# Whole-row taps of the last convolution tiles moved to ScalarE and added by transfers, in a kernel of attention and 7x7 depthwise convolution

## The chip, the cores and the metric

The kernel runs on one core of a Trainium2 chip. Times are microseconds of device time for one execution. The kernel before took 2925.66 us, the median of three runs.

## The reference

The input x has 16 images of 384 channels and 32 x 32 pixels in float32. Two layers follow each other, both with a residual and a GroupNorm of 32 groups ahead (`_gn`; its scale is one and its shift is zero):

```
x = x + attention(_gn(x))       # 8 heads of 48, 1024 tokens, softmax, projection with bias
x = x + depthwise_7x7(_gn(x))   # one 7x7 filter per channel, made symmetric under rotation
```

The filter is the mean of the weight and its three rotations by 90 degrees. The convolution pads with three zeros on each side, so its 49 taps (dy, dx) run from -3 to 3 in both directions, and a tap with dy = 2 touches 30 of the 32 rows.

## The kernel before

**Tiles.** The 384 channels are three tiles k = 0, 1, 2 of 128 partitions, each with the 1024 pixels of one image along the free dimension (512 KB). A tile is named (b, k), so that (15, 0) is the first tile of the last image. Attention works on four units (pairs of heads) per image. TensorE is busy with it nearly all the time: scores (L469), values times scores (L485), q and k (L418), v (L444), projection (L538). ScalarE takes the exponentials (L477) and copies results out of PSUM. The projection is added to x by an accumulating transfer issued on POOL (L553), which gives the tile `x1`.

**The convolution on VectorE.** It runs one image behind attention. `conv_begin` applies the GroupNorm to x1 and gives `xn1`. `conv_tap` (L600) is one instruction per tap: it multiplies a shifted window of xn1 by one weight per channel and adds it into x1. When the 49 taps of a tile are done, `conv_end` (L610) stores it from POOL's queue.

**The last tiles.** After the last attention unit there is nothing left to hide a convolution behind, so the last six tiles are shared out:

- (14, 2), (15, 2) and (15, 1), `PE_TILES`, go to TensorE. `conv_store` (L674) writes xn1 to a padded scratch in HBM, `conv_load` (L681) reads it back as tiles `sh` in which shifted rows lie on other partitions (four transfers of 160 KB, two each from SP's and ScalarE's queues in the tail), and `conv_on_pe` (L704) multiplies them by matrices made of the weights: seven column shifts dx, in two groups d0 of rows, 14 groups for each half of the image. For (14, 2) and (15, 2), `conv_on_pe_end` copies the sum out on ScalarE (L719), adds it into x1 by an accumulating transfer on POOL (L720), and stores. For (15, 1), `conv_on_pe_half` adds each half on VectorE (L727) and stores it (L728).
- (14, 0), (14, 1) and (15, 0) stay on VectorE. The last of them, `LONE`, alternates between two accumulators, x1 and `sum2`[...]; L858 starts sum2 and L866 joins the two at the end.

**Order.** The program is one long sequence that a planner in the kernel's Python code writes out. `clock` is its estimate of TensorE's time and `vclock` of VectorE's; `catch_up` issues taps until vclock reaches clock, and work that is due later sits in the heap `later`, each entry with a due time and a cost in microseconds. `applies` holds work for ScalarE that `act_slot` puts between exponentials. `fast_finish` writes the last projection of an image, its divisions included (L566 holds the reciprocal that VectorE takes first), and sets vclock anew. `fast_end` computes the statistics of the last x1 on TensorE (L308, with L327 and L330 on VectorE and the power L329 on POOL), applies them (L336 on VectorE and on POOL, L340 on ScalarE) and starts the last chains. Every engine, and every engine's transfer queue, works in the order in which it was written: an instruction that waits holds back all that stand behind it on that engine. Buffers come from pools: `epool` 8, `opool` 6, `npool` 6 for xn1, `tpool` 2.

Of the kernel before, what the change touches and what calls it, by code (L numbers as in the profile page):

```python
# [10 lines left out]
F32 = mybir.dt.float32  # L11
I32 = mybir.dt.int32
AF = mybir.ActivationFunctionType
ALU = mybir.AluOpType
AX = mybir.AxisListType

P = 128
# [27 lines left out]
def kernel(  # L45
# [25 lines left out]
    nc = tc.nc  # L71

    B, C, H, W = x.shape
    N = H * W
    NK = C // P
# [3 lines left out]
    HALF = N // 2  # L79
    KS = w_conv.shape[2]  # L80
    PAD = KS // 2
# [6 lines left out]
    TAPS = sorted(  # L88
        ((i - PAD, j - PAD) for i in range(KS) for j in range(KS)), key=lambda t: t != (0, 0)
    )  # L90
# [3 lines left out]
    wsym = consts.tile([P, NK, KS, KS], F32, name="wsym")  # L94
# [15 lines left out]
    def run(general):  # L110
        tag = "g" if general else "f"
        with ExitStack() as stack:
# [26 lines left out]

            PE_TILES = [(B - 2, PE_K[0])] + [(B - 1, k) for k in PE_K]  # L140
            LONE = (B - 1, 0)

            def flat(t):
                return t.rearrange("p h n -> p (h n)")
# [441 lines left out]
                )  # L586


            def region(*ds):
                return [(slice(max(0, -d), H - max(0, d)), slice(max(0, d), H - max(0, -d))) for d in ds]  # L590

            def conv_begin(st, b, k, engine):
                xn1s[b, k] = npool.tile([P, N], F32, tag="xn1", name=f"xn1_{b}_{k}")
                st.apply(xn1s[b, k], x1s[b, k], k, engine)

            def conv_tap(b, k, dy, dx, dst=None):
                (oy, iy), (ox, ix) = region(dy, dx)
                dst = x1s[b, k] if dst is None else dst
                acc = dst.rearrange("p (h w) -> p h w", w=W)[:, oy, ox]
                nc.vector.scalar_tensor_tensor(  # L600
                    acc,
                    xn1s[b, k].rearrange("p (h w) -> p h w", w=W)[:, iy, ix],
                    wsym[:, k, dy + PAD, dx + PAD : dx + PAD + 1],
                    acc,
                    ALU.mult,
                    ALU.add,
                )

            def conv_end(b, k):
                nc.gpsimd.dma_start(  # L610
                    out[b, k * P : (k + 1) * P].rearrange("p h w -> p (h w)"), x1s.pop((b, k))
                )
# [63 lines left out]
            def conv_load(b, k, h, a):  # L676
# [11 lines left out]
                    )  # L688
                shs[b, k, h, a] = t

            def conv_on_pe(b, k, h, first, last):
                if (b, k) not in pss:
                    pss[b, k] = psum(f"ps_conv_{b}_{k}")
                order = sorted(
                    ((d0, dx) for d0 in range(2) for dx in range(-PAD, PAD + 1)),
                    key=lambda t: t[1] != 0,
                )
                for n, (d0, dx) in enumerate(order):
                    if not first <= n < last:
                        continue  # L700
                    _, (ox, ix) = region(0, dx)
                    for i in range(SH):
                        src = shs[b, k, h, i // 2][:, i % 2, 0 : ROWS * W]
                        nc.tensor.matmul(  # L704
                            pss[b, k][CH * i : CH * (i + 1), h, :].rearrange(
                                "p (y x) -> p y x", x=W
                            )[:, :, ox],
                            lhsT=mats[k][:, i, d0 * KS + dx + PAD, :],
                            rhs=src.rearrange("p (y x) -> p y x", x=W)[
                                :, SH * d0 : SH * d0 + H // 2, ix  # L710
                            ],
                            start=(n == 0),
                            stop=(n == len(order) - 1),
                        )

            def conv_on_pe_end(b, k):

                t = tpool.tile([P, N], F32, tag="t", name=f"conv_{b}_{k}")
                nc.scalar.copy(t, flat(pss.pop((b, k))))  # L719
                nc.gpsimd.dma_start(x1s[b, k], t, accum_op=ALU.add)  # L720
                conv_end(b, k)

            def conv_on_pe_half(b, k, h):

                c = slice(h * HALF, (h + 1) * HALF)
                dst = x1s[b, k][:, c]
                nc.vector.tensor_tensor(dst, pss[b, k][:, h, :], dst, ALU.add)  # L727
                (nc.gpsimd, nc.sync)[h].dma_start(  # L728
                    out[b, k * P : (k + 1) * P].rearrange("p h w -> p (h w)")[:, c], dst
                )  # L730
# [88 lines left out]
            def now():  # L819
                return vclock if catching else max(clock, vclock)  # L820

            def after(wait, cost, f):

                nonlocal count
                count += 1
                heapq.heappush(later, (now() + wait, count, cost, f))

            def us_tap(dy, dx):
                late_us = 0.02 if clock > last_image else 0.0
                return ((H - abs(dy)) * (W - abs(dx)) + (128 if len(active) > 1 else 268)) / 955 + late_us  # L830

            def tap():

                while len(active) < NK and chains:
                    active.append([*chains.popleft(), 0])
                if not active:
                    return 0.0
                b, k, n = active[0]
                if (b, k) == LONE:
                    active.append(active.pop(0))  # L840
                    return tap_of_two(b, k, active[-1])
                took = us_tap(*TAPS[n])
                conv_tap(b, k, *TAPS[n])
                c = active.pop(0)
                c[2] += 1
                if c[2] < len(TAPS):
                    active.append(c)
                else:
                    conv_end(b, k)
                return took  # L850

            def tap_of_two(b, k, c):

                n = c[2]
                c[2] += 1
                if n == 1:
                    late["sum2"] = opool.tile([P, N], F32, tag="o", name=f"sum2_{b}_{k}")
                    nc.vector.tensor_scalar(  # L858
                        late["sum2"], xn1s[b, k], wsym[:, k, PAD, PAD : PAD + 1], None, ALU.mult
                    )  # L860
                elif n < len(TAPS):

                    tn = n if n > 1 else 1
                    conv_tap(b, k, *TAPS[tn], late["sum2"] if n % 2 else None)
                else:
                    nc.vector.tensor_tensor(x1s[b, k], x1s[b, k], late["sum2"], ALU.add)  # L866
                    active.remove(c)
                    conv_end(b, k)
                return (950 + 128) / 955

            def catch_up(to):
                nonlocal vclock, catching
# [114 lines left out]
                    f()  # L987

            def x1_chains(b, st):
                on_pe = [t for t in PE_TILES if t[0] == b]  # L990
                for k in range(NK - 1, -1, -1):
                    conv_begin(st, b, k, (nc.gpsimd, None, nc.vector)[k] if b == B - 1 else None)
                    if (b, k) in on_pe:
                        conv_store(b, k)

                        cuts = (0, KS, KS + 2, KS + 4, 2 * KS) if b == B - 2 else (0, KS, 2 * KS)
                        pe_conv.extend((b, k, 0, *c) for c in zip(cuts, cuts[1:]))
                        pe_conv.extend((b, k, 1, n, n + KS) for n in (0, KS))
                after(
                    2.0 if b == B - 1 else 6.0,  # L1000
                    0.0,
                    lambda: chains.extend(
                        (b, k) for k in range(NK) if (b, k) not in on_pe
                    ),
                )
# [114 lines left out]
            def conv_piece():  # L1120
                nonlocal clock
                b, k, h, first, last = pe_conv.popleft()
                while (b, k, h, 1) not in shs and pe_loads:
                    loads(1)
                conv_on_pe(b, k, h, first, last)
                clock += 6.2 * (last - first) / KS
                if last == 2 * KS:
                    loads(2)
                    if (b, k) == PE_TILES[-1]:
                        after(6.0, 0.7, lambda: conv_on_pe_half(b, k, h))  # L1130
                    elif h == 1:
                        after(6.0, 1.2, lambda: conv_on_pe_end(b, k))
# [29 lines left out]
                vclock = clock + 4.0  # L1162

            def fast_end(b):

                x1_stats[b].groups_on_pe(late["masks"], tap, conv_piece)
                conv_piece()
                x1_chains(b, x1_stats[b])
# [140 lines left out]
```

## Time and profile before

| what | us |
|---|---|
| median of three runs | 2925.66 |
| lowest, highest of them | 2924.74, 2926.32 |
| profiled execution, own time | 2926.36 |
| profiled execution, span of the core | 2924.6 |
| TensorE busy (share of the span) | 2895.0 (99%) |
| VectorE busy | 2580.3 (88%) |
| ScalarE busy | 1441.0 (49%) |
| POOL busy | 254.2 (9%) |
| transfers by POOL, queue q0, share of 16 engines | 14.7% |

The span is what the trace shows of the core, from its first to its last instruction; the execution's own time is 1.8 us more. All times in the timelines count from the start of the span. The last stage begins near 2832, when attention's matmuls end, and lasts to 2924.6. A row of a timeline gives the start, the duration, the engine, the line, the operation and its tiles, and in brackets how long the engine was idle before it and what ended that. A transfer's row gives the time that its issue took on the queue; the views of transfers give the time from issue to landing.

### The profile page before, as it was taken

To read this page: it belongs to the slowest core of one execution; us is meant where nothing else is said; L and a number is where in the kernel's file an instruction comes from. 1 tells how busy PE (TensorE), PEld (TensorE's weight loads), DVE (VectorE), ACT (ScalarE), POOL (GpSimd) and SP (SyncE) were. 2 spreads that over 40 slices of the span, in tenths; PEclk is the share of its full clock that TensorE was granted. 3 is DMA by queue.
4 is the path that set the end of the run, shared out by engine and by line. 5 is a ranking of instruction groups with operands and counts; after the bars stand their busy time and mean duration, and the time that the engine had idled before them with its cause. 6 is when DMAs were issued, how large, how long until landed. Compare 5 with 4: busy or idle time off the path is not lost.

```text
span 2924.6 us, 30111 instructions
## 1 busy us (share of the span) xinstructions
PE 2895.0 (99%) x11442; PEld 1164.5 (40%) x11442; DVE 2580.3 (88%) x2571; ACT 1441.0 (49%) x1721; POOL 254.2 (9%) x400
## 2 busy tenths in 40 slices
PE   8999999999999999999999999999999999999997
PEld 4343343433434343343433434343343434434332
DVE  5312999989899898999989899898999989899988
ACT  2545445464454655445464454556445464554520
POOL 3111004010100101000010100101010010100000
PEclk9999999999999999999999999999999999999999
DMA  7422022120312203012220302203022220302314
GB/s 281 131 29 62 16 35 76 37 68 23 68 29 43 69 21 84 16 35 69 42 63 23 72 29 39 70 21 84 16 41 64 43 62 24 80 24 35 104 53 128
DMA packets 72059, 168.93 MB, mean 58 GB/s; under 512 B 30288, under 2 KB 32224, under 8 KB 70368
## 3 DMA queue, kind: packets, MB, share of 16 engines
q0 software_dynamic: 32688, 109.34, 14.7%
q1 hardware_dynamic: 37936, 54.94, 7.4%
q10 hardware_dynamic: 1280, 2.62, 0.3%
q8 instruction: 92, 1.51, 0.2%
q14 instruction: 63, 0.52, 0.1%
HBM read 118.61 MB, written 28.72 MB: 50 GB/s over the span
## 4 chain that ended last, share of the span: by engine, by line
PE 92%; issue 5%; DVE 2%; DMA 0%; POOL 0%; ACT 0%; POOLq 0%
PE ps_s L469 29%; PE acc L485 29%; PE ps_qk L418 17%; PE ps_v L444 9%; PE ps_proj L538 8%; DVE x L600 1%; DVE sum L600 1%; DMA x<-in_x 0%; PE warm L1060 0%; PE ps_st_x L308 0%; ACT qk L425 0%; POOL v L180 0%; POOL qk L434 0%; POOL sc_x L329 0%; POOL x L1241 0%
## 5 line engine op out<-in xcount | busy, mean ns | idle before, releaser
L600 DVE SCALAR_TENSOR_TENSOR x<-xn,wsym,x 128x899 f32<-128x899 f32 (+9 forms) x2181 | 2375.7, 1162 | 138.7 <-ACT xn L340 138.7
L477 ACT ACTIVATE e<-ps_s 128x1024 f32<-128x1024 f32 x1024 | 952.4, 1051 | 52.2 <-PE ps_s L469 49.1
L469 PE MATMUL ps_s<-qk 48*128 48x512 f32 x4096 | 914.8, 596 | 1.3 <-ACT qk L425 1.1
L485 PE MATMUL acc<-e,v 128*64 128x512 f32 x4096 | 907.2, 595 | 0.0
L469 PEld LDWEIGHTS ps_s<-qk 48*128 48x128 f32 x4096 | 375.9, 185 | 536.4 <-ACT e L477 259.6
L485 PEld LDWEIGHTS acc<-e,v 128*64 128x64 f32 x4096 | 283.0, 137 | 608.2 <-issue 600.8
L418 PE MATMUL ps_qk<-x,wqk 128*128 128x512 f32 x1152 | 508.7, 598 | 2.4 <-DVE x L336 2.4
L496 ACT COPY o<-acc 128x512 f32<-128x512 f32 x128 | 75.1, 587 | 604.7 <-PE acc L485 604.7
L418 PEld LDWEIGHTS ps_qk<-x,wqk 128*128 128x128 f32 x1152 | 217.2, 191 | 290.1 <-issue 287.6
L444 PE MATMUL ps_v<-wv,x 128*128 128x384 f32 x768 | 252.0, 488 | 0.0
L538 PE MATMUL ps_proj<-o,wp 128*128 128x512 f32 x540 | 234.2, 592 | 0.0
L425 ACT COPY qk<-ps_qk 128x1024 f32<-128x1024 f32 x96 | 96.9, 1009 | 263.6 <-PE ps_qk L418 263.6
L553 POOL DMA_DIRECT2D x<-in_x x45 | 39.4, 875 | 1803.0 <-ACT x L546 1424.3
L444 PEld LDWEIGHTS ps_v<-wv,x 128*128 128x128 f32 x768 | 144.6, 190 | 109.6 <-ACT e L477 12.1
L538 PEld LDWEIGHTS ps_proj<-o,wp 128*128 128x128 f32 x540 | 102.6, 190 | 126.0 <-issue 119.6
L453 ACT COPY v<-ps_v 128x384 f32<-128x384 f32 x128 | 55.1, 483 | 185.5 <-PE ps_v L444 185.5
L546 ACT ACTIVATE x<-ps_proj,bp 128x1024 f32<-128x1024 f32 x45 | 50.2, 1114 | 182.7 <-PE ps_proj L538 182.7
L521 DVE TENSOR_TENSOR o<-o,inv 128x1024 f32<-128x1024 f32 x63 | 76.8, 1219 | 51.0 <-DMA inv<-inv 46.5
L340 ACT ACTIVATE xn<-x,sc_x 128x1024 f32<-128x1024 f32 x46 | 53.8, 1231 | 80.3 <-DMA sc_x<-gr_x 57.0
L704 PE MATMUL ps_conv<-sh,mat 128*32 128x464 f32 (+3 forms) x672 | 69.2, 570 | 1.9 <-DVE x L727 1.9
L363 DVE BATCH_NORM_STATS2 bs_all<-xs 128x6 f32<-128x512 f32 x84 | 52.2, 683 | 18.2 <-DMA xs<-in_x 18.2
L510 DVE RECIPROCAL rec<-sums 128x16 f32<-128x16 f32 x63 | 15.3, 243 | 53.6 <-DMA sums<-sum 53.5
(123 smaller groups left out, 556.6 us busy)
## 6 DMA issues: line engine op xcount, KB each, us to landing
x<-in_x POOLq DMA_DIRECT2D x90, 512.0 KB, 5.6
inv<-inv SPq DMA_DIRECT2D x126, 256.0 KB
out<-x POOLq DMA_DIRECT2D x47, 512.0 KB, 3.8
xs<-in_x POOLq DMA_DIRECT2D x42, 512.0 KB, 6.5
qk<-qk POOLq DMA_DIRECT2D x96, 128.0 KB, 5.8
o<-o SPq DMA_DIRECT2D x90, 64.0 KB
sh<-xd SPq DMA_DIRECT2D x32, 160.0 KB
x<-in_x SPq DMA_DIRECT2D x6, 512.0 KB
```

Of the source, the lines that this page charges most:

```text
L418: nc.tensor.matmul(ps[:, h, :], lhsT=wqk[:, k, s, t, :], rhs=xns[b][:, k, h * HALF : (h + 1) * HALF], start=(k == 0), stop=(k == NK - 1),)
L425: nc.scalar.copy(halves(qks[u][:, s, :]), ps)
L444: nc.tensor.matmul(ps[:, j, 0:C], lhsT=xns[b][:, k, t * P : (t + 1) * P], rhs=wv[:, k, :], start=(k == 0), stop=(k == NK - 1),)
L453: nc.scalar.copy(dst.rearrange("p (h d) -> p h d", d=D + 1)[:, :, 0:D], ps[:, j, 0:C].rearrange("p (h d) -> p h d", d=D),)
L469: nc.tensor.matmul(ps[:, j, :], lhsT=qks[u][r, 1, i * P : (i + 1) * P], rhs=qks[u][r, 0, h * HALF : (h + 1) * HALF], start=True, stop=True,)
L477: nc.scalar.activation(es[n], ps, AF.Exp, scale=SCALE)
L485: nc.tensor.matmul(accs[u, h][64 * j : 64 * j + 64, :], lhsT=v_of(u, i, j), rhs=e[:, j, :], start=(i == 0), stop=(i == NT - 1),)
L496: nc.scalar.copy(os_[u][:, h * HALF : (h + 1) * HALF], accs.pop((u, h)))
L521: nc.vector.tensor_tensor(os_[u], os_[u], invs.pop(u), ALU.mult)
L538: nc.tensor.matmul(ps[:, h, :], lhsT=wp[:, t, o * P : (o + 1) * P], rhs=os_[NP * b + t][:, h * HALF : (h + 1) * HALF], start=(t == 0), sto ...
L600: nc.vector.scalar_tensor_tensor(acc, xn1s[b, k].rearrange("p (h w) -> p h w", w=W)[:, iy, ix], wsym[:, k, dy + PAD, dx + PAD : dx + PAD + 1],
L704: nc.tensor.matmul(pss[b, k][CH * i : CH * (i + 1), h, :].rearrange("p (y x) -> p y x", x=W)[:, :, ox], lhsT=mats[k][:, i, d0 * KS + dx + ...
```

## The change

A tap with dx = 0 covers whole rows: its product is one contiguous run, weight times xn1 shifted by dy rows. The change takes such taps (`ROWS_ONLY`) off TensorE and VectorE. ScalarE computes the product into a buffer (`product`), and an accumulating transfer from POOL's queue adds it into the tile (`add_rows`).

- The three PE_TILES give up dy = 1, 2, 3. `PE_TAPS` therefore has 13 groups, not 14 (the second row group at dx = 0 is gone). For (14, 2) the three products are made during the last attention, in buffers of xn1 that are still spare (`rows_early`); for (15, 2) and (15, 1) in the tail, in two buffers of opool and one of npool each.
- (14, 1) gives up dy = -1, 1, 2, with products made before the last apply.
- LONE gives up all seven taps with dx = 0. Two products start sum2 and a new accumulator `sum3` (`lone_sums`); five are added into sum3 by transfers, one after the other. At the end VectorE adds sum3 to sum2 and sum2 to x1, in halves, each stored at once, one from SP's queue and one from ScalarE's.
- `add_step` works through the additions of the four tiles in turn, one from each. The sum of a tile on TensorE is taken only after its additions are written (`late["pe"]`), and (14, 1) is stored after its third addition.
- The apply of (15, 0) moves from POOL to ScalarE.
- `vclock -= 5.0` makes the planner place more taps ahead of the last image's reciprocals.

VectorE's taps in the whole program go from 2204 to 2195, and those behind the last apply from 60 to 48. The diff without its asserts and blank lines:

```diff
@@ -139,6 +139,13 @@
     PE_TILES = [(B - 2, PE_K[0])] + [(B - 1, k) for k in PE_K]
     LONE = (B - 1, 0)
+    ROWS_ONLY = {bk: (1, 2, 3) for bk in PE_TILES}
+    ROWS_ONLY[B - 2, 1] = (-1, 1, 2)
+    ROWS_ONLY[LONE] = range(-PAD, PAD + 1)
+    def taps_of(b, k):
+        return [t for t in TAPS if t[1] or t[0] not in ROWS_ONLY.get((b, k), ())]
     def flat(t):
         return t.rearrange("p h n -> p (h n)")
@@ -586,11 +593,27 @@
         )
+    spare = {}
+    def new_xn1(b, k):
+        return npool.tile([P, N], F32, tag="xn1", name=f"xn1_{b}_{k}")
+    def product(dst, b, k, dy):
+        rows, src = ((slice(i.start * W, i.stop * W)) for i in region(dy)[0])
+        nc.scalar.activation(
+            dst[:, rows],
+            xn1s[b, k][:, src],
+            AF.Identity,
+            scale=wsym[:, k, dy + PAD, PAD : PAD + 1],
+        )
+        return dst[:, rows], rows
     def region(*ds):
         return [(slice(max(0, -d), H - max(0, d)), slice(max(0, d), H - max(0, -d))) for d in ds]
     def conv_begin(st, b, k, engine):
-        xn1s[b, k] = npool.tile([P, N], F32, tag="xn1", name=f"xn1_{b}_{k}")
+        xn1s[b, k] = spare.pop((b, k), None) or new_xn1(b, k)
         st.apply(xn1s[b, k], x1s[b, k], k, engine)
     def conv_tap(b, k, dy, dx, dst=None):
@@ -688,14 +711,14 @@
             )
         shs[b, k, h, a] = t
+    PE_TAPS = [(d0, dx) for d0 in range(2) for dx in range(-PAD, PAD + 1) if d0 == 0 or dx]
+    PE_TAPS.sort(key=lambda t: t[1] != 0)
     def conv_on_pe(b, k, h, first, last):
         if (b, k) not in pss:
             pss[b, k] = psum(f"ps_conv_{b}_{k}")
-        order = sorted(
-            ((d0, dx) for d0 in range(2) for dx in range(-PAD, PAD + 1)),
-            key=lambda t: t[1] != 0,
-        )
-        for n, (d0, dx) in enumerate(order):
+        for n, (d0, dx) in enumerate(PE_TAPS):
             if not first <= n < last:
                 continue
             _, (ox, ix) = region(0, dx)
@@ -710,11 +733,12 @@
                         :, SH * d0 : SH * d0 + H // 2, ix
                     ],
                     start=(n == 0),
-                    stop=(n == len(order) - 1),
+                    stop=(n == len(PE_TAPS) - 1),
                 )
     def conv_on_pe_end(b, k):
         t = tpool.tile([P, N], F32, tag="t", name=f"conv_{b}_{k}")
         nc.scalar.copy(t, flat(pss.pop((b, k))))
         nc.gpsimd.dma_start(x1s[b, k], t, accum_op=ALU.add)
@@ -722,6 +746,7 @@
     def conv_on_pe_half(b, k, h):
         c = slice(h * HALF, (h + 1) * HALF)
         dst = x1s[b, k][:, c]
         nc.vector.tensor_tensor(dst, pss[b, k][:, h, :], dst, ALU.add)
@@ -839,12 +864,15 @@
         if (b, k) == LONE:
             active.append(active.pop(0))
             return tap_of_two(b, k, active[-1])
-        took = us_tap(*TAPS[n])
-        conv_tap(b, k, *TAPS[n])
+        taps = taps_of(b, k)
+        took = us_tap(*taps[n])
+        conv_tap(b, k, *taps[n])
         c = active.pop(0)
         c[2] += 1
-        if c[2] < len(TAPS):
+        if c[2] < len(taps):
             active.append(c)
+        elif (b, k) in ROWS_ONLY:
+            late["done"] = (b, k)
         else:
             conv_end(b, k)
         return took
@@ -853,20 +881,82 @@
         n = c[2]
         c[2] += 1
-        if n == 1:
-            late["sum2"] = opool.tile([P, N], F32, tag="o", name=f"sum2_{b}_{k}")
-            nc.vector.tensor_scalar(
-                late["sum2"], xn1s[b, k], wsym[:, k, PAD, PAD : PAD + 1], None, ALU.mult
-            )
-        elif n < len(TAPS):
-            tn = n if n > 1 else 1
-            conv_tap(b, k, *TAPS[tn], late["sum2"] if n % 2 else None)
+        taps = taps_of(b, k)
+        if n < len(taps):
+            conv_tap(b, k, *taps[n], late["sum2"] if n % 2 else None)
+        elif n == len(taps):
+            dst = late["sum2"]
+            nc.vector.tensor_tensor(dst, dst, late["sum3"], ALU.add)
         else:
-            nc.vector.tensor_tensor(x1s[b, k], x1s[b, k], late["sum2"], ALU.add)
+            for h in range(2):
+                cols = slice(h * HALF, (h + 1) * HALF)
+                dst = x1s[b, k][:, cols]
+                nc.vector.tensor_tensor(dst, dst, late["sum2"][:, cols], ALU.add)
+                (nc.sync, nc.scalar)[h].dma_start(
+                    out[b, k * P : (k + 1) * P].rearrange("p h w -> p (h w)")[:, cols], dst
+                )
             active.remove(c)
-            conv_end(b, k)
         return (950 + 128) / 955
+    adds = deque()
+    def add_step(due):
+        nonlocal count
+        todo, finally_do = adds.popleft()
+        add_rows(*todo.pop(0))
+        if todo:
+            adds.append((todo, finally_do))
+        else:
+            finally_do()
+        if adds:
+            due += max(2.2, 8.0 / len(adds))
+            count += 1
+            heapq.heappush(later, (due, count, 0.0, lambda: add_step(due)))
+    def add_rows(b, k, t, rows):
+        dst = late["sum3"] if (b, k) == LONE else x1s[b, k]
+        nc.gpsimd.dma_start(dst[:, rows], t, accum_op=ALU.add)
+    def rows_early(b, k, n, dy):
+        t, rows = product(spare[B - 1, n % NK], b, k, dy)
+        add_rows(b, k, t, rows)
+    def rows_late(b, k, dys, tiles):
+        return [(b, k, *product(tiles(), b, k, dy)) for dy in dys]
+    def e_tile():
+        return flat(epool.tile([P, 2, HALF], F32, tag="e", name="e_tap"))
+    def o_tile():
+        return opool.tile([P, N], F32, tag="o", name="o_tap")
+    def xn1_tile():
+        return npool.tile([P, N], F32, tag="xn1", name="xn1_tap")
+    def lone_sums(b, k):
+        product(late["sum2"], b, k, 0)
+        product(late["sum3"], b, k, 1)
+    def end_rows():
+        def nothing():
+            late["pe"] = late.get("pe", 0) + 1
+        def done():
+            conv_end(*late["done"])
+        adds.append((late["rows"], done))
+        adds.append((rows_late(*LONE, (-1, 2, -2, 3, -3), e_tile), lambda: None))
+        for bk in PE_TILES[1:]:
+            free = [o_tile, o_tile, xn1_tile]
+            adds.append((rows_late(*bk, ROWS_ONLY[bk], lambda: free.pop(0)()), nothing))
+        add_step(now())
     def catch_up(to):
         nonlocal vclock, catching
@@ -987,15 +1077,33 @@
             f()
     def x1_chains(b, st):
+        nonlocal vclock
         on_pe = [t for t in PE_TILES if t[0] == b]
         for k in range(NK - 1, -1, -1):
-            conv_begin(st, b, k, (nc.gpsimd, None, nc.vector)[k] if b == B - 1 else None)
+            conv_begin(st, b, k, nc.vector if (b, k) == (B - 1, NK - 1) else None)
             if (b, k) in on_pe:
                 conv_store(b, k)
-                cuts = (0, KS, KS + 2, KS + 4, 2 * KS) if b == B - 2 else (0, KS, 2 * KS)
+                cuts = (0, KS, KS + 2, KS + 4) if b == B - 2 else (0, KS)
+                cuts = (*cuts, len(PE_TAPS))
                 pe_conv.extend((b, k, 0, *c) for c in zip(cuts, cuts[1:]))
-                pe_conv.extend((b, k, 1, n, n + KS) for n in (0, KS))
+                pe_conv.extend(((b, k, 1, 0, KS), (b, k, 1, KS, len(PE_TAPS))))
+        if b == B - 1:
+            lone_sums(*LONE)
+            after(2.5, 0.0, end_rows)
+        if b == B - 2:
+            vclock -= 5.0
+            for k in range(NK):
+                spare[B - 1, k] = new_xn1(B - 1, k)
+            for n, dy in enumerate(ROWS_ONLY[PE_TILES[0]]):
+                applies.append(
+                    (
+                        clock + 9.0 + 7.0 * n,
+                        1.3,
+                        lambda n=n, dy=dy: rows_early(*PE_TILES[0], n, dy),
+                    )
+                )
         after(
             2.0 if b == B - 1 else 6.0,
             0.0,
@@ -1124,7 +1232,7 @@
             loads(1)
         conv_on_pe(b, k, h, first, last)
         clock += 6.2 * (last - first) / KS
-        if last == 2 * KS:
+        if last == len(PE_TAPS):
             loads(2)
             if (b, k) == PE_TILES[-1]:
                 after(6.0, 0.7, lambda: conv_on_pe_half(b, k, h))
@@ -1162,6 +1270,11 @@
         vclock = clock + 4.0
     def fast_end(b):
+        late["rows"] = rows_late(b - 1, 1, ROWS_ONLY[b - 1, 1], e_tile)
+        for key in ("sum2", "sum3"):
+            late[key] = opool.tile([P, N], F32, tag="o", name=key)
+        nc.gpsimd.memset(late["sum3"][:, N - W :], 0.0)
         x1_stats[b].groups_on_pe(late["masks"], tap, conv_piece)
         conv_piece()
```

## What was predicted

> **What bounds the kernel now.** I read the page first, its busy shares and the transfer queues, then the last 90 us engine by engine, because the change touches nothing before the last two images.
>
> ```profile
> PE 2895.0 (99%) x11442; PEld 1164.5 (40%) x11442; DVE 2580.3 (88%) x2571; ACT 1441.0 (49%) x1721; POOL 254.2 (9%) x400
> ...
> q0 software_dynamic: 32688, 109.34, 14.7%
> ```
>
> TensorE is full over the span, yet the end is not its own. VectorE's timeline from the last GroupNorm apply (columns: start, duration, instruction):
>
> ```profile
> 2844.45 0.81 DVE L336 TENSOR_SCALAR xn<-x,sc_x 128x1024 f32<-128x1024 f32 x1
> 2845.17 5.01 DVE L600 SCALAR_TENSOR_TENSOR x<-xn,wsym,x 128x870 f32<-128x870 f32 x4
> ...
> 2899.74 0.67 DVE L727 TENSOR_TENSOR x<-ps_conv,x 128x512 f32<-128x512 f32 x1
> ...
> 2912.07 0.67 DVE L727 TENSOR_TENSOR x<-ps_conv,x 128x512 f32<-128x512 f32 x1
> 2912.67 1.07 DVE L600 SCALAR_TENSOR_TENSOR x<-xn,wsym,x 128x841 f32<-128x841 f32 x1
> 2913.78 1.23 DVE L866 TENSOR_TENSOR x<-x,sum 128x1024 f32<-128x1024 f32 x1
> ```
>
> No idle is printed after the apply: VectorE works 2844.45 to 2915.0 in one piece and sets the end. TensorE's convolution matmuls (L704) end at 2906.3. POOL then issues the last store:
>
> ```profile
> 2844.52 2.68 POOL L336 TENSOR_SCALAR xn<-x,sc_x 128x1024 f32<-128x1024 f32 x1 [0.31 <-DVE sc_x L330]
> ...
> 2876.96 0.91 POOL L720 DMA_DIRECT2D x<-conv  x1 [11.33 <-issue]
> 2882.67 0.55 POOL L610 DMA_DIRECT2D out<-x  x1 [4.80 <-DMA x<-conv]
> ...
> 2915.30 0.53 POOL L610 DMA_DIRECT2D out<-x  x1 [14.05 <-DVE x L866]
> ```
>
> It lands 3.7 us later, at 2919.0; the span ends 5.6 us after that, which no part of the change shortens. The table by stage shows who has room (DMA share is the last but one column):
>
> ```profile
> core 0: us, PE busy (x) PEld busy (x) DVE busy (x) ACT busy (x) POOL busy (x), PEclk, DMA share, GB/s
> 2846.00:2858.00 12.00, 12.00 (x124) 3.81 (x116) 12.00 (x18) 0.00 (x0) 1.20 (x1) 1.00 0.68 198
> 2858.00:2870.00 12.00, 12.00 (x126) 3.93 (x122) 11.97 (x15) 0.00 (x0) 1.16 (x2) 1.00 0.68 199
> 2870.00:2882.00 12.00, 12.00 (x124) 3.81 (x116) 12.00 (x11) 1.01 (x1) 0.91 (x1) 1.00 0.64 155
> 2882.00:2894.00 12.00, 12.00 (x124) 3.90 (x120) 12.00 (x12) 1.01 (x1) 1.77 (x3) 1.00 0.77 199
> 2894.00:2906.00 12.00, 10.12 (x104) 2.94 (x96) 12.00 (x13) 0.00 (x0) 0.75 (x2) 1.00 0.17 68
> ```
>
> ScalarE is free. The transfer engines are not: they are two thirds busy until 2894, though their mean over the kernel is low.
>
> **What the Trainium skill says.** "Trainium Kernel Development and Optimization", Key Constraints: transfers issued by SP, ACT and POOL all run on the same 16 engines and interleave. The trace agrees: between 2859 and 2868.3 a batch of loads and two stores from different queues fill 8.1 us of the engines, the 5.5 that such a batch takes alone (2850 to 2856.4) plus two stores of 1.3. "DMA: Bandwidth & Descriptors", SWDGE vs HWDGE vs iDMA: accumulation during a transfer is issued from GpSimd only; here every accumulate (L553, L720) is on POOL. Same page, Rules for kernel authors: an accumulate reads its destination and writes it later, and another write landing in between is lost; so additions into one tile go one after the other, each waiting for the last to land. The trace shows this once: the store at 2882.67 waited 4.80 us for x<-conv. Same page, Anatomy of one DMA: some 2.0 us of a transfer are fixed. Here it is a little more, as the next view shows. Queue q0 alone in the stretch 2877.2 to 2881.4 (one 512 KB accumulate) and in 2915 to 2920 (one 512 KB store):
>
> ```profile
> q0 software_dynamic: 142, 0.52, 63.4%
> ...
> x<-conv POOLq DMA_DIRECT2D x1, 512.0 KB, 5.2
> ```
>
> ```profile
> q0 software_dynamic: 144, 0.52, 26.2%
> ...
> out<-x POOLq DMA_DIRECT2D x1, 512.0 KB, 3.7
> ```
>
> An accumulate holds the engines 0.634 x 4.2 = 2.66 us and lands after 5.2; so 2.5 us of it are no work. A store holds them 0.262 x 5 = 1.31 us.
>
> **The change, part by part.**
>
> *TensorE.* One of 14 tap groups goes: 48 of 672 records of L704. At 0.108 us a record (72.4 us of work from 2832.05 to 2906.3) that is -5.2 us: end at 2901.
>
> *VectorE.* After the last apply 60 taps (54,534 elements) become 48 (43,409). Taps follow each other at (elements + 118)/955 us (992: 1.16; 841: 1.00), so 64.5 becomes 51.4: -13.1. L858 goes (-0.7), joining sum2 and sum3 comes (+1.2 like L866), the last sum in two halves costs 2 x 0.67 against 1.23 (+0.1). Net -12.5: 2915.0 becomes 2902.5. Three of the 12 taps run ahead of the first reciprocal, which waits 4.60 us at 2803.28 anyway: free.
>
> *New wait 1.* The first tap on x1_14_1 after the apply waits for an accumulate that POOL issues only behind the power L329 (ends 2844.2). Landing 5.1 to 6.0 (L553's spread) gives 2849.3 to 2850.2 against a tap due at 2845.2: 4 to 5 us, and all of VectorE's queue stands behind it. I take 5: end 2907.5.
>
> *New wait 2.* The first half-sum of (15,1) (L727 before) now waits for TensorE's last matmul and three accumulates; three taps, the join, both half-sums of the last tile and the other half of (15,1) stand behind it: 0.6 + 3.2 + 1.2 + 1.3 + 0.6 = 6.9 us. 2901 + 6.9 = 2908. This and wait 1 run side by side, they do not add.
>
> *ScalarE.* Three early products stand between copies of ScalarE; 0 to 1.25 us each on TensorE; I take 0, since ScalarE is 49% busy and TensorE waited 1.1 us in all for such copies (L469 for ACT qk L425). Three more lie in its 23.25 us of idle before the apply L340. Then come two sums, the apply taken from POOL, and eleven products at 1.25 us; behind them on ScalarE's queue stand its issues of the second batch of loads (sh<-xd), 2863.6 instead of 2858.6. TensorE has its first half to work on meanwhile; if that cover fails, up to 5 us.
>
> *POOL.* 14 accumulates at 0.9 us of issue are 12.6 us where POOL was 6.3 us busy: not its work but its order counts. Its apply (2.68) goes, hidden before. Accumulates and stores are in one queue, and at four places POOL waits for a landing: the third addition of (14,1), the convolution of (14,2), the third of sum3, the convolution of (15,2). The last addition of sum3, for which the last join waits, stands behind all of these.
>
> *Transfers.* The 14 additions move 2944 elements a partition for (14,1), 4768 for sum3, 2880 each for (15,2) and (15,1): 13,472, or 13.2 tiles of 1024, at 2.66: **35.0 us** of all engines. Free of them between 2846 and 2906 (12 us times one less the share): 3.8 + 3.8 + 4.3 + 2.8 + 10.0 = 24.7 us. The rest, 10.3 us, runs past 2906 to 2916.3, or 2914.8 since the first addition can start 1.5 us ahead of 2846. That is with engines never idle. I add 1.0 while ScalarE makes the products and two of the four landing waits uncovered by other queues, 2 x 2.5 (bounds none and all four, 0 and 10); the last landing comes about 1.0 after the data: 2921.8. Then the join 1.2, two half-sums 1.3, and a 256 KB store at the 3.1 us of L728: 2927.4. Against 2919.0: **+8.4 us**. VectorE, ready at 2908, waits some 13 us.
>
> The profiled execution took 2926.36 us, its span 2924.6 plus 1.8 around it; 0.7 above the median 2925.66. So 2934.8 in its terms, **2934.0** in the median's.
>
> **Rivals.**
> (A) *Additions hidden.* If adjoining accumulates overlap inside an engine and cost 1.4 us or less of it, 13.2 x 1.4 = 18.5 fits in the 24.7 free, and sum3 lands by 2905.3, before VectorE's 2908. Then 2908.5 + 3.1 = 2911.6: -7.4, or 2918.3. For it: the lone accumulate comes in bursts with holes. Against: I counted busy time, not the holes. It decides from sum3 landing before about 2906.
> (B) *Middle.* An accumulate at 2.0 us: 26.4 in all, 8.6 less than above; sum3 lands at 2913.2, and 5.6 us later the store: 2918.8, or -0.2: 2925.5. The late loads of the second batch (up to 5 us on TensorE, so 2908 becomes 2913) lead to the same place.
> (C) *Queues share alike.* If additions slow the loads of sh that TensorE needs and all four landing waits show, 5 us more: +13.4, 2939.
> (D) *The taps do not move.* Excluded as far as the instruction order goes: it shows the 48 taps and all 14 additions.
>
> **How the numbers follow.** Additions as the bound at 2.3 to 2.7 us each: 0.40; (C) 0.13; (B) 0.20; (A) 0.27. A measurement of this kernel can tell some 0.2%, 5.9 us: faster is below 2919.8, slower above 2931.5. Of the 0.40, whose low end is +3.8, about 0.05 stay within; (A) clears the bound by 1.5 us only, so 0.04 of it is within, and 0.02 of (B) is faster. Faster 0.25, within 0.27, slower 0.48. The range takes in (A) and (C): 2917.5 to 2940. The likeliest case's own is 2929 to 2937.
>
> **What would show it.** Right: VectorE idle for over 8 us shortly before the join, released by a transfer into sum3; transfer share above 0.85 from 2858 on; the last store near 2924. Wait 1: 4 to 5 us idle near 2845, released by x<-e_tap. Wrong: transfer share under 0.8 with sum3 landed by 2906, or a join waiting on nothing. If the half-sum of (15,1) shows the long wait on TensorE instead, the loads were late, not the additions.

## The result and the profile after

The changed kernel takes 2930.99 us (median of 19 runs, 2930.02 to 2932.43) against 2925.66 us: the ratio is 1.0019 with a 95% interval of 1.0012 to 1.0026. It is slower by 5.3 us; the forecast was 2934.0, 8.4 slower. By the prediction's own bound of 5.9 us this counts as "within", to which it gave 0.27, and not as "slower", to which it gave 0.48. The difference is real all the same: the 19 runs of the kernel before end at 2926.70, below the lowest of the change. Its profiled execution took 2932.39 us, with a span of 2930.3.

VectorE's timeline after (start, duration, instruction, and in brackets its idle time and what ended it):

```profile
2843.77 0.85 DVE L343 TENSOR_SCALAR xn<-x,sc_x 128x1024 f32<-128x1024 f32 x1
2850.07 4.23 DVE L623 SCALAR_TENSOR_TENSOR x<-xn,wsym,x 128x870 f32<-128x870 f32 x4 [5.46 <-DMA x<-e_tap]
...
2909.68 0.69 DVE L752 TENSOR_TENSOR x<-ps_conv,x 128x512 f32<-128x512 f32 x1 [9.92 <-DMA x<-xn_tap]
...
2921.47 1.23 DVE L890 TENSOR_TENSOR sum<-sum,sum 128x1024 f32<-128x1024 f32 x1 [7.99 <-DMA sum<-e_tap]
2922.73 1.29 DVE L896 TENSOR_TENSOR x<-x,sum 128x512 f32<-128x512 f32 x2
2923.94 0.68 DVE L752 TENSOR_TENSOR x<-ps_conv,x 128x512 f32<-128x512 f32 x1
```

Where VectorE had no idle before, it now has three holes, 23.4 us together, and a transfer ends each. The taps did go: the 48 that are left are over at 2913.5. What it waits for at the end is the fifth addition into sum3. POOL's queue shows why that comes so late:

```profile
2843.51 1.20 POOL L922 DMA_DIRECT2D x<-e_tap  x1
...
2875.59 0.85 POOL L922 DMA_DIRECT2D x<-e_tap  x1 [2.64 <-DMA x<-e_tap]
2893.08 0.56 POOL L633 DMA_DIRECT2D out<-x  x1 [16.64 <-DMA x<-e_tap]
2893.63 0.90 POOL L744 DMA_DIRECT2D x<-conv  x1
...
2907.26 0.86 POOL L744 DMA_DIRECT2D x<-conv  x1 [1.74 <-DMA x<-xn_tap]
2915.73 0.56 POOL L633 DMA_DIRECT2D out<-x  x1 [7.61 <-DMA x<-conv]
2916.28 0.89 POOL L922 DMA_DIRECT2D sum<-e_tap  x1
```

The store of (14,1) stands in the queue behind an addition that took 17.2 us to land, and everything else on POOL stands behind the store: in the 16.6 us that POOL waited there it issued nothing. The table by stage (the last column but one is the transfer engines' share) shows both sides of it:

```profile
core 0: us, PE busy (x) PEld busy (x) DVE busy (x) ACT busy (x) POOL busy (x), PEclk, DMA share, GB/s
...
2858.00:2870.00 12.00, 10.98 (x108) 4.20 (x112) 11.97 (x14) 6.00 (x7) 4.68 (x6) 1.00 1.07 232
2870.00:2882.00 12.00, 10.55 (x104) 3.64 (x96) 12.00 (x12) 1.01 (x1) 1.93 (x3) 1.00 1.06 274
2882.00:2894.00 12.00, 9.52 (x80) 3.55 (x84) 12.00 (x12) 1.01 (x1) 0.92 (x2) 0.86 0.78 186
2894.00:2906.00 12.00, 12.00 (x124) 4.55 (x118) 5.75 (x6) 0.00 (x0) 4.61 (x6) 1.00 0.85 211
2906.00:2918.00 12.00, 1.46 (x12) 0.26 (x4) 3.80 (x4) 0.00 (x0) 2.86 (x4) 0.78 0.76 167
```

From 2858 to 2882 the engines are full. From 2882 to 2918 they have work left and stand idle a fifth of the time, because POOL may not issue it. TensorE is hit too: its convolution, 48 records shorter, ends at 2907.5, not earlier than before. It waited for late loads of sh, as the waits of this stage say (the last three numbers are the time in all, the number of waits and the longest):

```profile
POOL out L633 <- DMA x<-e_tap: 16.6, 1, 16.6
...
PE ps_conv L727 <- DMA sh<-xd: 5.8, 2, 3.9
```

The second of these waits ends at 2884.5, and behind it TensorE's granted clock was low for a while: the table has 0.86 for this stage, with 80 records in 9.5 busy us where the next stage has 124 in 12. By the next stage's rate some 98 would have fitted, so an estimate from these counts is 1.7 us lost.

### The profile page after: what moved, and what is told of

The parts are those of the page before. It is cut to its first block, busy times and chain, and to the rows that moved or that the text cites. A ratio compares the mean times of both kernels' runs of the same rounds, so it can differ in the third digit from the quotient of the medians.

```text
span 2930.3 us, 30050 instructions
## 1 busy us (share of the span) xinstructions
PE 2892.4 (99%) x11394; PEld 1165.4 (40%) x11394; DVE 2570.1 (88%) x2563; ACT 1460.8 (50%) x1741; POOL 266.5 (9%) x416
## 4 chain that ended last, share of the span: by engine, by line
PE 93%; issue 4%; DMA 2%; POOL 0%; DVE 0%; ACT 0%; POOLq 0%; DVEq 0%
PE ps_s L476 30%; PE acc L492 29%; PE ps_qk L425 17%; PE ps_v L451 9%; PE ps_proj L545 8%; DMA x<-e_tap 1%; DMA x<-conv 0%; DMA x<-xn_tap 0%; DMA sum<-e_tap 0%; PE ps_st_x L315 0%; PE warm L1168 0%; POOL v L187 0%; POOL x L922 0%; POOL sc_x L336 0%; POOL out L633 0%
## 5 line engine op out<-in xcount | busy, mean ns | idle before, releaser
L623 DVE SCALAR_TENSOR_TENSOR x<-xn,wsym,x 128x960 f32<-128x960 f32 (+9 forms) x2174 | 2367.2, 1164 | 142.5 <-ACT xn L347 137.1
L347 ACT ACTIVATE x<-x,x_sc 128x1024 f32<-128x1024 f32 x42 | 51.1, 1271 | 20.1 <-DMA x<-in_x 19.9
```

Source lines behind the costliest of these rows:

```text
L347: nc.scalar.activation(dst, src, AF.Identity, bias=self.sc[:, k, 1:2], scale=self.sc[:, k, 0:1],)
L623: nc.vector.scalar_tensor_tensor(acc, xn1s[b, k].rearrange("p (h w) -> p h w", w=W)[:, iy, ix], wsym[:, k, dy + PAD, dx + PAD : dx + PAD + 1],
```

## The experiments

Each experiment's difference is taken to the kernel before as run beside it on the same chip.

| kernel | median us | to before | ratio, 95% interval |
|---|---|---|---|
| the change | 2930.99 | +5.3 | 1.0019 [1.0012, 1.0026] |
| e1_short_adds | 2913.68 | -11.8 | 0.9960 [0.9946, 0.9974] |
| e2_stores_later | 2921.58 | -3.9 | 0.9988 [0.9979, 0.9996] |
| e3_store_pool | 2936.64 | +11.2 | 1.0037 [1.0024, 1.0051] |
| e4_before_store | 2921.15 | -4.3 | 0.9985 [0.9978, 0.9991] |
| e5_no_141 | 2919.89 | -5.0 | 0.9982 [0.9974, 0.9991] |
| e6_no_late_pe | 2916.14 | -8.8 | 0.9970 [0.9958, 0.9981] |
| e7_both_less | 2916.83 | -8.1 | 0.9971 [0.9960, 0.9981] |
| e8_before_ahead | 2922.66 | -2.3 | 0.9992 [0.9984, 1.0000] |
| e9_ahead_half_later | 2918.82 | -6.7 | 0.9977 [0.9968, 0.9987] |
| e10_halves_last | 2914.62 | -10.9 | 0.9962 [0.9948, 0.9975] |
| e11_half_later | 2932.97 | +7.4 | 1.0025 [1.0015, 1.0035] |

### Bytes or order: e1_short_adds and e2_stores_later

```diff
-                nc.gpsimd.dma_start(dst[:, rows], t, accum_op=ALU.add)
+                nc.gpsimd.dma_start(
+                    dst[:, rows.start : rows.start + W], t[:, 0:W], accum_op=ALU.add
+                )
```

> The changed kernel, but each of the additions of row products moves 32 columns instead of 928 to 992 (the rest of each product is left out). Number, order and waits of the additions stay, their bytes go. Theory (engine time of the transfers is the bound, 35 us of it): the last sum3 addition lands before VectorE's taps end, the join waits for less than 2 us, VectorE ends near 2908.5, and with the 5.7 us that follow it in the changed kernel and 2.1 around the span the time is 2914 to 2919. Rival (the chain of landings and POOL's order hold the end, whatever the bytes): the join still waits over 5 us, 2925 or more.

VectorE's timeline of e1_short_adds:

```profile
2898.48 0.69 DVE L752 TENSOR_TENSOR x<-ps_conv,x 128x512 f32<-128x512 f32 x1 [1.99 <-PE ps_conv L727]
...
2902.36 1.23 DVE L890 TENSOR_TENSOR sum<-sum,sum 128x1024 f32<-128x1024 f32 x1
```

With 14 additions in the same order but hardly any bytes, the join waits for nothing and the half-sum waits 2 us for TensorE, which now ends at 2898.4 and has no wait for sh left, although ScalarE still makes all the products ahead of the loads. The time is 17.1 us below the change's in differences to before, a little more than the theory's range. The bytes of the additions are therefore the root; the fixed part of 14 landings is not.

Queue q0 in the stretch 2846 to 2918, in the changed kernel and in e1_short_adds:

```profile
q0 software_dynamic: 2667, 9.36, 59.0%
```

```profile
q0 software_dynamic: 2816, 3.62, 21.0%
```

0.590 x 72 us is 42.5 us of all engines. Less two convolution sums at 2.66 and four stores at 1.31 it leaves 31.9. The 9.36 MB less 0.52 for each of these six leave 6.2 MB of additions, or 12.0 tiles: about 2.7 us a tile, the size that the prediction used.

In e2_stores_later only three stores move in POOL's queue:

```diff
                 def done():
-                    conv_end(*late["done"])
+                    after(20.0, 0.0, lambda: conv_end(*late["done"]))
...
                 nc.gpsimd.dma_start(x1s[b, k], t, accum_op=ALU.add)
-                conv_end(b, k)
+                after(9.0, 0.0, lambda: conv_end(b, k))
```

> The changed kernel with the three stores that make POOL wait for a landing written later: (14,1) by 20 planned us, (14,2) and (15,2) by 9, so that additions issue ahead of them; same transfers, same bytes. Theory of engine time alone: the engines were full, so at most 1.5 us are gained: 2929.5 to 2931. Rival (order: the 16.6 us at which POOL stood before the store of (14,1), and 7.6 before that of (15,2), left the engines a quarter idle from 2882 to 2918): sum3 lands at 2914 to 2917 instead of 2921.5, time 2924 to 2927.

It gains 9.2 us over the change, more than either side expected. The table by stage of e2_stores_later, and its VectorE:

```profile
2882.00:2894.00 12.00, 10.90 (x108) 4.29 (x112) 12.00 (x12) 1.01 (x1) 1.71 (x2) 1.00 1.07 253
2894.00:2906.00 12.00, 10.62 (x100) 3.90 (x96) 6.40 (x7) 0.00 (x0) 3.66 (x5) 1.00 1.05 252
```

```profile
2904.65 0.69 DVE L752 TENSOR_TENSOR x<-ps_conv,x 128x512 f32<-128x512 f32 x1 [5.60 <-PE ps_conv L727]
...
2910.10 1.22 DVE L890 TENSOR_TENSOR sum<-sum,sum 128x1024 f32<-128x1024 f32 x1 [1.65 <-issue]
```

The engines now stay full until 2906, and the join runs 11.4 us earlier. So there are two layers: the additions fill the engines, and in the change POOL's order also left them idle. Without the second layer the change, in this order of VectorE's instructions, still brings nothing beyond its stores: e2_stores_later is at -3.9, e4_before_store (below) at -4.3.

### The last store: e3_store_pool and e4_before_store

e3_store_pool goes back from the two halves to one sum and one POOL store; e4_before_store puts the halves, and nothing else, into the kernel before:

```diff
-                    nc.vector.tensor_tensor(x1s[b, k], x1s[b, k], late["sum2"], ALU.add)
+                    for h in range(2):
+                        cols = slice(h * HALF, (h + 1) * HALF)
+                        dst = x1s[b, k][:, cols]
+                        nc.vector.tensor_tensor(dst, dst, late["sum2"][:, cols], ALU.add)
+                        (nc.sync, nc.scalar)[h].dma_start(
+                            out[b, k * P : (k + 1) * P].rearrange("p h w -> p (h w)")[:, cols], dst
+                        )
                     active.remove(c)
-                    conv_end(b, k)
```

> The changed kernel with the last sum and store as before: one VectorE addition of 1024, one 512 KB store from POOL. As the prediction costed it (landing 3.7 instead of 3.1, the end 5.6 us after the landing in both): +0.5 to +1, 2931.5 to 2932. Rival (the 2.4 us that the prediction was too high at the end come from the queue of the last store: the span ends 3.4 us after the last data where SP and ACT store, 6 where POOL does): +2.5 to +4, 2933.5 to 2935.

> The kernel before with only the last sum and store in halves, stored from SP's and ScalarE's queues. As the prediction costed it: -0.5 to -1, 2924.7 to 2925.2. Rival (the end after a last store from POOL is longer by over 2 us): -2.5 to -4, 2921.7 to 2923.2.

Both went the rival's way and beyond its range: +5.9 against the change, -4.3 against before. The last sum and the span of e3_store_pool, then of e4_before_store:

```profile
core 0 of [0], span 2935.4 us
...
2922.07 1.23 DVE L893 TENSOR_TENSOR x<-x,sum 128x1024 f32<-128x1024 f32 x1
2923.21 0.68 DVE L752 TENSOR_TENSOR x<-ps_conv,x 128x512 f32<-128x512 f32 x1
```

```profile
core 0 of [0], span 2919.5 us
...
2913.01 1.29 DVE L869 TENSOR_TENSOR x<-x,sum 128x512 f32<-128x512 f32 x2
```

From VectorE's last instruction to the end of the span it is 11.5 us with POOL's store (2923.9 to 2935.4; 9.6 in the kernel before) and 5.2 us with SP's and ScalarE's (2914.3 to 2919.5; 5.7 in the change). Only part of it is the data: in e3_store_pool they have moved by 2927.0, and the span ends 8.4 us later; in e4_before_store by 2916.5, and 3.0 later. Both edits change two things at once, the queue and the split of one store into two, and no run parts them. The traces speak for the queue without showing it: in all thirteen the span ends 9.3 us or more after the start of the last store on POOL, and in e7_both_less, where that store has only 256 KB, it ends 9.6 us after it (2903.4 to 2913.0). What holds the end in the POOL case was not tried.

### Which additions pay: e5_no_141, e6_no_late_pe, e7_both_less

All three start from e2_stores_later. e5_no_141 drops the additions of (14,1):

```diff
-            ROWS_ONLY[B - 2, 1] = (-1, 1, 2)
...
-                adds.append((late["rows"], done))
...
-                late["rows"] = rows_late(b - 1, 1, ROWS_ONLY[b - 1, 1], e_tile)
```

> e2_stores_later without the three row additions of (14,1): three taps go back to VectorE (+3.2 us), its 5.8 us wait for the first addition goes, and the transfers lose 2944 of 13472 elements a partition, 7.7 us of engine time. If engine time still holds back loads and the sum of three (e2_stores_later: transfer share 1.05 until 2906): both gains count, 2915 to 2919 against 2921.6. Rival (VectorE is now held by TensorE's last matmul alone): no change within 1 us, 2920.5 to 2922.5.

It falls between the two: 1.1 us better than e2_stores_later. The first wait is gone, but the first half-sum has come to stand earlier in VectorE's queue and idles 6.46 us for TensorE at 2899.51. As a test of the engine time alone it is inconclusive.

e6_no_late_pe keeps (14,1) and drops the additions of (15,2) and (15,1), which go back to TensorE with 14 groups:

```diff
-            ROWS_ONLY = {bk: (1, 2, 3) for bk in PE_TILES}
+            ROWS_ONLY = {bk: (1, 2, 3) for bk in PE_TILES[:1]}
...
-                for bk in PE_TILES[1:]:
+                for bk in PE_TILES[1:1]:
```

> e2_stores_later without the six row additions of (15,2) and (15,1): TensorE keeps their 32 records more (+3.5 us of its own work), the transfers lose 15 us. If the additions cost TensorE more in late loads than they save it: it ends near 2902 instead of 2904.6, the half-sum follows at once, 2914 to 2917. Rival (TensorE's own work counts): it ends at 2908, 2919 to 2923.

It is 4.9 us better than e2_stores_later in differences to before, as the theory had it, with *more* work on TensorE, whose last matmul ends at 2903.1 instead of 2904.6:

```profile
2903.16 0.69 DVE L756 TENSOR_TENSOR x<-ps_conv,x 128x512 f32<-128x512 f32 x1 [2.50 <-PE ps_conv L733]
2903.77 1.22 DVE L894 TENSOR_TENSOR sum<-sum,sum 128x1024 f32<-128x1024 f32 x1
```

TensorE's waits for sh fall from 5.7 us to 1.7, which pays for the 32 records that came back (and its convolution happens to start 0.6 us earlier in this trace). The six additions thus cost TensorE at least what they saved it. Only 1.5 us of the gain are TensorE's, however. Three taps that stood behind the half-sum in e2_stores_later now stand ahead of it (3.2 us), and the join no longer idles 1.65 us: VectorE ends 6.3 us earlier, of which a longer stretch behind it (7.3 us instead of 5.9) takes 1.4 back.

e7_both_less drops those of (14,1) and (15,1), and writes the first half-sum later (this part of its edit alone is shown):

```diff
-                        after(6.0, 0.7, lambda: conv_on_pe_half(b, k, h))
+                        after(12.0 if h == 0 else 6.0, 0.7, lambda: conv_on_pe_half(b, k, h))
```

> e2_stores_later without the additions of (14,1) and of (15,1), and the first half-sum of (15,1) written 6 planned us later so that taps no longer stand behind it. Transfers lose 15.4 us. VectorE without waits: 2902.5 + 3.2 = 2905.7 at its end; TensorE near 2900. From VectorE's end another 5.7 us and 2.1 around the span: 2913 to 2916, the best so far. Rival (sum3's five landings in a row hold the join anyway): 2917 to 2921.

At 2916.83 it just misses its range on the high side. The join waits for nothing, so the rival is out; the half-sum still idles 3.03 us for TensorE.

### The half-sum's place: e8 to e11

e8_before_ahead is e4_before_store with the step back of the planner's clock:

```diff
             def x1_chains(b, st):
+                nonlocal vclock
+                if b == B - 2:
+                    vclock -= 5.0
```

> e4_before_store with the planner's step back of 5 us ahead of the last image's reciprocals, no other part of the change. Three taps run in a 4.6 us wait of VectorE instead of in the tail: -3.2 us if VectorE still sets the end, 2917 to 2919 against 2921.2. Rival (the later reciprocals hold the last projection): 0 or slower, 2921 to 2924.

It is 2.0 us *slower* than e4_before_store. Three taps do run ahead of the first reciprocal, and attention's end does not move (TensorE's last stretch of convolution starts at 2831.2 in e4_before_store, 2831.3 here). The rival named the wrong cause too. VectorE of e8_before_ahead:

```profile
2898.07 1.17 DVE L600 SCALAR_TENSOR_TENSOR sum<-xn,wsym,sum 128x930 f32<-128x930 f32 x1
2903.60 0.69 DVE L727 TENSOR_TENSOR x<-ps_conv,x 128x512 f32<-128x512 f32 x1 [4.36 <-PE ps_conv L704]
2904.20 1.15 DVE L600 SCALAR_TENSOR_TENSOR x<-xn,wsym,x 128x900 f32<-128x900 f32 x1
```

In the kernel before, the first half-sum was written ahead of TensorE's last 56 records, which waited 1.9 us for it:

```profile
2900.47 5.82 PE L704 MATMUL ps_conv<-sh,mat 128*32 128x464 f32 x56 [1.89 <-DVE x L727]
```

With the clock moved it is written behind them: VectorE waits 4.4 us and nine taps stand behind. e9_ahead_half_later moves it:

```diff
-                        after(6.0, 0.7, lambda: conv_on_pe_half(b, k, h))
+                        after(14.0 if h == 0 else 6.0, 0.7, lambda: conv_on_pe_half(b, k, h))
```

> e8_before_ahead with the first half-sum of (15,1) written 8 planned us later, so that two taps, not nine, stand behind its wait for TensorE's last matmul. If that order took the gain of the taps run ahead (e8: 4.4 us idle before the half-sum against 3 taps saved): VectorE ends near 2911.2 instead of 2915.6, 2917.5 to 2919.5 against 2922.7. Rival (the taps run ahead delay attention's end): no change, 2922 to 2923.5.

It takes 2918.82 us: the gain of the taps is back, -2.4 us against e4_before_store. So the order was the cause.

e10_halves_last is e7_both_less with both half-sums behind the join and the last sum:

```diff
-                        after(12.0 if h == 0 else 6.0, 0.7, lambda: conv_on_pe_half(b, k, h))
+                        after(24.0 if h == 0 else 18.0, 0.7, lambda: conv_on_pe_half(b, k, h))
...
-                (nc.gpsimd, nc.sync)[h].dma_start(
+                (nc.scalar, nc.sync)[h].dma_start(
```

> e7_both_less with the join and the last sum written ahead of both half-sums of (15,1), whose first half is stored from ScalarE's queue. VectorE no longer idles 3.0 us ahead of them: it ends when TensorE has ended plus two half-sums, 2902.4 + 1.3 = 2903.7 instead of 2906.1: -2.4, 2913 to 2915.5 against 2916.8. Rival (sum3 lands late and holds the join, or four stores of 256 KB at once at the end take longer): within 1 us of e7_both_less.

```profile
2900.77 1.08 DVE L622 SCALAR_TENSOR_TENSOR sum<-xn,wsym,sum 128x841 f32<-128x841 f32 x1
2901.94 1.22 DVE L894 TENSOR_TENSOR sum<-sum,sum 128x1024 f32<-128x1024 f32 x1
2903.20 1.29 DVE L900 TENSOR_TENSOR x<-x,sum 128x512 f32<-128x512 f32 x2
2904.64 1.29 DVE L756 TENSOR_TENSOR x<-ps_conv,x 128x512 f32<-128x512 f32 x2
```

No idle is left on VectorE from the apply to the end. At 2914.62 us it is the fastest kernel here apart from e1_short_adds, which leaves most of the products out: 10.9 us below the kernel before, 16.2 below the change. Its runs overlap with those of e7_both_less (2912.67 to 2915.18 against 2913.70 to 2918.22), so the step from one to the other is not sharp. Against e9_ahead_half_later, which has the stores, the step back and a later half-sum but no additions, the rest of the change with the eight late additions that are left brings 4.2 us.

e11_half_later makes the same move in the changed kernel itself:

> The changed kernel with both half-sums of (15,1) written behind the join and the last sum (the first stored from ScalarE's queue). Its 9.9 us wait no longer holds back taps. Theory (the fifth landing of sum3 sets the end alone): nothing gained, the join still waits until 2921 and one more half-sum stands behind it: 2930.5 to 2932.5. Rival (the half-sum's wait counts as well): 2928 or less.

```profile
2920.39 1.22 DVE L890 TENSOR_TENSOR sum<-sum,sum 128x1024 f32<-128x1024 f32 x1 [17.29 <-DMA sum<-e_tap]
```

The 9.92 us wait is gone, and the join's has grown from 7.99 to 17.29: VectorE has less to do and waits longer for the same landing. The time is 2.1 us above the change's, 0.5 above the expected range. With the additions as they are, the half-sum's wait costs nothing.

## Why the prediction was right, and where its steps failed

- **The bound.** Right. The join waits for the fifth landing of sum3, at 2921.4 (forecast 2921.8), and the transfer engines are what makes it late (e1_short_adds). An addition holds them about 2.7 us a tile (forecast 2.66). The forecast's only trace of the wait between accumulates is a store (2882.67); POOL's queue after shows it for additions, with 2.64 us ahead of 2875.59.
- **How the lateness is made up.** Right in sum, wrong in kind. The step "two of the four landing waits uncovered by other queues, 2 x 2.5" took a landing wait at the length that a lone accumulate shows. Full engines stretched one landing to 17.2 us, and POOL stood 16.6 us at that place alone. e2_stores_later puts that order at 9.2 us. From 2882 to 2918 the engines idled 7.3 us (12 us times one less the share), where 6.0 were allowed for another reason: that the landing came within 0.4 us is in part luck. The sign "transfer share above 0.85 from 2858 on" failed with it: 0.78, 0.85 and 0.76 from 2882.
- **New wait 1.** Right: 5.46 us against 5.
- **New wait 2.** Its place was right, its releaser only in part: the last addition of (15,1) landed 2.2 us after TensorE's end. The other 7.7 us are a wait for TensorE, the forecast's sign that the loads were late: they were, beside the additions. The wait was counted at no cost beside the join, which e11_half_later confirms.
- **TensorE.** "-5.2 us: end at 2901" failed: it ended at 2907.5, since the cover for the late loads, named as the thing that could fail, did fail. The trace shows 5.8 us of waits for sh and some 1.7 of a low clock against the 5.2 saved, and e6_no_late_pe that TensorE ends no later without six additions. The forecast saw the danger in ScalarE's queue, where the loads stand behind the products; e1_short_adds has that queue too and no such wait, so the full engines made the loads late.
- **The end after the last store.** This is the term that made the number too high. "The span ends 5.6 us after that, which no part of the change shortens", with 3.1 us for the store itself, came to 8.7 us from the last sum of the last tile. Measured, it is 6.3 (2924.0 to 2930.3), 2.4 less. The change did shorten it, by its last store, which is now two halves from SP's and ScalarE's queues: e3_store_pool and e4_before_store put this at 5.9 and 4.3 us. For the profiled execution the forecast is 2.4 us too high (2934.8 against 2932.39), which is this term. The other 0.6 us between forecast and median is that this execution lay 1.4 us above its median, not 0.7. The forecast's "slower by 8.4" was thus right in its last landing (about 2927) and wrong in what follows it.
- **The taps run ahead.** "Free" failed as a general statement: in e8_before_ahead they cost 2.0 us net, by moving the half-sum in the written order. In the change this was hidden behind sum3.

The sum of parts, in differences to before: the last store, as measured in the kernel before, gives -4.3; everything else in the change costs +9.6, of which POOL's order is 9.2. What is left of the whole shift of taps is then about nothing. Had the additions carried hardly any bytes, it would have gained 7.5 us (e1_short_adds at -11.8, less the 4.3 of the last store).

## What to carry to other kernels

Before moving work to transfers, add up the busy time of all the transfer engines in the stage where they are to run, from a lone transfer of the same kind, and compare it with what is free there: the mean share over the kernel says nothing. In a queue with waits, write what someone waits for last ahead of what only has to be stored, since under load a landing can take three times its lone length (17.2 us here, against 5.2 for a lone one). When taps or steps are moved in a sequence written by a planner, look again at the order of the instructions with waits, because their places move too.

## What the runs showed that was not expected

The two kernels that store the last sum from POOL ended 9.6 and 11.5 us after VectorE's last instruction, the eleven that store it from SP and ScalarE 5.2 to 7.3 us after it. The longest of these, 6.8 to 7.3, are e6_no_late_pe, e7_both_less and e10_halves_last; the reason was not tried.

Full transfer engines show a share of 1.05 to 1.07 in the records: no stage of 12 us in the tables here goes above that, while a landing took up to 17.2 us. In these runs a share near 1 was thus the limit, and not an overlap to be had for free.
